# Gathered columns of a graph layer wait for TensorE's banks and picks of the preceding unit

## The chip, the cores and the metric

One Trainium2 chip; the kernel runs on one of its cores. The metric is the device time of one execution in microseconds (us), the median of several runs. Engines are named as the profile names them: PE is TensorE, DVE is VectorE, ACT is ScalarE, POOL is GpSimd, SP is SyncE.

## What is computed

A layer of a graph network over 6250 nodes with 64 features and 206250 edges, sorted by their target node. Cut to what matters:

```python
h = jnp.maximum(_layernorm(x, axis=-1), 0.0)
msg = jax.nn.relu(h[src] + edge_attr)          # 206250 x 64
agg = jax.ops.segment_sum(msg, dst, num_segments=6250)
out = x + (jax.nn.relu((h + agg) @ W1 + b1) @ W2 + b2)
```

The costly part is `h[src]`, one row of 64 floats for each edge, the rows in no order.

## The kernel before

**Groups and units.** The edges are worked through in groups of 768 (128 partitions, 6 columns of edges), 268 whole groups and a short last one. After a prologue (layer norm, ranks, the first five groups) a loop runs over 276 units, one call of `half(u)` each. A unit fetches the rows of `h` in two ways. Three of a group's six columns are gathered: POOL issues one indirect DMA for each column, 128 rows of 256 bytes from the table `h_rows` in memory to a tile `xg` (`gather`, line 200). The other three are picked by TensorE out of a copy of `h` that lies on the chip as three bf16 parts (`hp`). A few groups (`WHOLE`) have all six columns picked, in two units; they have no gathers.

**What a unit does on TensorE**, in this order: `window_sum(u - 1)` (line 600) sums the messages of the unit before into a bank, 12 small matmuls. `slots_of` (line 487) fills three slot banks for the next set of picks: two `first` ones and one `later`, of 20, 16 and 16 matmuls. `pick(u + 1)` (line 502) picks rows with 18 matmuls. ACT copies each slot bank out (`slots_out`, line 495), puts the edge attributes into the pick bank (`room`, line 510), and makes the messages (line 590). The DVE adds a finished sum into the accumulator `z` (line 563), adds the gathered rows to the edge attributes (line 585), adds the three picked parts up (line 588), compares for the one-hot tiles (line 569), and makes the selection matrices `backs` (line 474) and `found` (line 455) for later units.

**Order.** The order of the instructions on each engine is that of the program's text, without a scheduler. The framework puts semaphore waits where data or buffers need them. `enter(g + AHEAD)` at the start of a unit loads the group nine ahead (`AHEAD = 9`): its edge attributes by SP, its gathers by POOL. The gathered tiles come from a ring of twelve (`LOOK = 12`). POOL has nothing else to do in the loop, so what holds a gather there is the ring alone: the first column of a group waits for line 585 of the group that last used its buffer.

Of the kernel before, what the change touches and what calls it, by code (L numbers as in the profile page):

```python
# [21 lines left out]
G = 6  # L22
# [17 lines left out]
AHEAD = 9  # L40
# [4 lines left out]
H = 3  # L45
PP, RR = 128, 49
# [4 lines left out]
S = 32  # L51
J = P // S
assert PARTS * BB == RR - 1 and PP == P and PARTS % J == 0
Q = PARTS * S // P
# [3 lines left out]
RAW = 3  # L58
# [23 lines left out]
def kernel(  # L82
# [14 lines left out]
    nc = tc.nc  # L97
# [9 lines left out]
    src_sb = const.tile([P, CP], I32, name="src_sb")  # L107
# [70 lines left out]
    hp = const.tile([PP, RR, 3, D], BF16, name="hp")  # L178

    h_rows = dram.tile([NP, D], F32, name="h_rows")  # L180
# [8 lines left out]
    def attr_load(ea, g):  # L189
        if g < NG:  # L190
            nc.sync.dma_start(out=ea.rearrange("p j d -> p (j d)"),
                              in_=edge_attr[g * GE:(g + 1) * GE, :].rearrange("(p j) d -> p (j d)", j=G))
        else:
            nc.sync.dma_start(out=ea[:, G - CT:G - 1].rearrange("p j d -> p (j d)"),
                              in_=edge_attr[C * P:(C + TJ) * P, :].rearrange("(p j) d -> p (j d)", j=TJ))
            nc.sync.dma_start(out=ea[:, G - 1, :], in_=edge_attr[E - P:, :])

    def gather(xg, idx, n, rows):
        for j in range(n):
            nc.gpsimd.indirect_dma_start(  # L200
                out=xg[:, j, :], out_offset=None, in_=rows[:, :],
                in_offset=bass.IndirectOffsetOnAxis(ap=idx[:, j:j + 1], axis=0))

    def first_col(g):
        return 0 if g < NG else G - CT

    def is_whole(g):
        return g in WHOLE

    def pool_cols(g):  # L210
        return G if g < F0 else 0 if is_whole(g) else G - H

    def load(g):
        ea = eas[g % LOOK]
        attr_load(ea[:, :G], g)
        lo, hi = first_col(g), pool_cols(g)
        if is_whole(g):
            return ea, None
        if g < F0:
            xg = lnp.tile([P, G, D], F32, name="xr", bufs=F0)  # L220
        else:
            xg = edge.tile([P, G - H, D], F32, name="xg")
        gather(xg[:, lo:], src_sb[:, g * G + lo:g * G + hi], hi - lo, x if g < RAW else h_rows)
        return ea, xg

    loaded = [load(g) for g in range(RAW)]
    tail_load(dst_sb, dst_tail)
    tail_load(src_sb, src_tail)
# [113 lines left out]
    def next_half():  # L342
        halves_made[0] += 1
        return half_banks[halves_made[0] % 3]
# [94 lines left out]
    backs, sources, spots, found, picked, halves, picks = {}, {}, {}, {}, {}, {}, {}  # L439

    def source_load(k):
        sources[k] = rank.tile([P, PARTS * 2 * S], I16, name="sources")
        nc.sync.dma_start(out=sources[k][:PP], in_=lines[k // SETS][k % SETS].rearrange("(o m) s -> o (m s)", o=1)
                          .to_broadcast([PP, PARTS * 2 * S]))

    def spot_load(k):
        spots[k] = rank.tile([P, 2 * H * P], BF16, name="spots")
        nc.sync.dma_start(out=spots[k], in_=spot_rows[k * 2 * H:(k + 1) * 2 * H, :]
                          .rearrange("(o t) s -> o (t s)", o=1).to_broadcast([P, 2 * H * P]))
# [16 lines left out]
    def back_near(k):  # L466
        nc.scalar.activation(backs[k][:, Q - 1].rearrange("p t s -> p (t s)"), dists.pop(k), AF.Relu,  # L467
                             bias=ones[:, 0:1], scale=-1.0)
# [10 lines left out]
    def slots_of(k, n0):  # L479
        ps = next_half()[:, :2 * 3 * D].rearrange("p (u d) -> p u d", u=2)  # L480
        for u in range(2):
            i, q = divmod(n0 + u, Q)
            sets = BB + 1 if q == 0 else BB
            for b in range(sets):
                for j in range(J):
                    m = (b * PARTS + q * J) + j if b < BB else BB * PARTS + j
                    nc.tensor.matmul(ps[j * S:(j + 1) * S, u], found[k][:, m, i, :],  # L487
                                     hp[:, min(m, RR - 1)].rearrange("p t d -> p (t d)"),
                                     start=(b == 0), stop=(b == sets - 1))
        if n0 == 0:  # L490
            picked[k] = hot.tile([P, 2 * Q, 3 * D], BF16, name="picked")
        halves[k, n0] = ps

    def slots_out(k, n0):
        nc.scalar.copy(picked[k][:, n0:n0 + 2], halves.pop((k, n0)))  # L495

    def pick(u0, cols):
        k, i = divmod(u0, 2)
        ps = picks[u0]
        for u in cols:  # L500
            for q in range(Q):
                nc.tensor.matmul(ps[:, u, :3].rearrange("p t d -> p (t d)"), backs[k][:, q, i * H + u, :],  # L502
                                 picked[k][:, i * Q + q], start=False, stop=(q == Q - 1), skip_group_check=True)

    def room(u):
        g, c0 = UNITS[u]
        picks[u] = pick_banks[u % 2]
        parts = taken[g][0][:, H:].rearrange("p (t c) d -> p c t d", c=H)
        if c0:
            nc.scalar.copy(picks[u][:, :H, :3], parts)  # L510
        else:
            nc.scalar.copy(picks[u][:, :H, 0], taken[g][0][:, :H])
            nc.scalar.copy(picks[u][:, :H, 1:3], parts[:, :, 1:])

    def group_of(u):
        return UNITS[u][0] if u >= 0 else F0 + u
# [4 lines left out]
    def is_first(u):  # L521
        return u <= 0 or UNITS[u - 1][0] != UNITS[u][0]
# [24 lines left out]
    aggs, hots, taken, msgs = {}, {}, {}, {}  # L547
# [13 lines left out]
    def sum_into_z(u):  # L561
        at = window_start(group_of(u))
        nc.vector.tensor_tensor(z[:, ds(at, W)], z[:, ds(at, W)], aggs.pop(u), ALU.add)  # L563
# [7 lines left out]
            slots.unsqueeze(1).to_broadcast([P, n, W]), ALU.is_equal)  # L571
        hots[u] = oh

    def enter(g):
        if g <= NG and g not in taken:
            taken[g] = loaded[g] if g < RAW else load(g)

    def messages(u):
        g, (lo, hi) = group_of(u), span(u)
# [15 lines left out]
    def window_sum(u):  # L595
        (lo, hi), oh, msg = span(u), hots.pop(u), msgs.pop(u)
        pa = half_banks[u % 3][:, 2 * 3 * D + u // 3 % AB * W:][:, :W]
        for j in range(lo, hi):
            i = (j - lo) % 2
            nc.tensor.matmul(pa[i * D:(i + 1) * D], msg[:, j, :], oh[:, j, :], start=(j < lo + 2), stop=(j >= hi - 2))  # L600
        aggs[u] = pa
# [41 lines left out]
    def blocks_behind(u):  # L643
        g = group_of(u)
        for c in sorted(res):
            store(c, *res.pop(c))
        for c in sorted(hid):
            res[c] = result(c, *hid.pop(c))
        for c in range(NB):
            if READY[c] == g and is_last(u):  # L650
                hid[c] = hidden(c)
# [6 lines left out]
    def is_set(k):  # L658
        return 0 <= k < KS

    def half(u):
        g = group_of(u)
        k, i = divmod(u, 2)
        first = ((0, 2), (6, 8))[i]
        later = ((4,), (10,))[i]
        now = is_set(k + 1)
        if is_first(u):
            enter(g + AHEAD)
        if i == 0:
            if is_set(k + 3):  # L670
                source_load(k + 3)
        elif is_set(k + 3):
            spot_load(k + 3)
        window_sum(u - 1)
        if u + 1 < U:
            room(u + 1)
        if now:
            for n0 in first:
                slots_of(k + 1, n0)
                slots_out(k + 1, n0)  # L680
            for n0 in later:
                slots_of(k + 1, n0)
        if u + 1 < U:
            pick(u + 1, range(H))
        sum_into_z(u - LAG)
        blocks_behind(u - LAG)
        messages(u)
        if now:
            for n0 in later:
                slots_out(k + 1, n0)  # L690
        one_hot(u)
        if i == 0:
            if is_set(k + 1):
                back_near(k + 1)
                back(k + 1, 3, Q)
            if is_set(k + 2):
                find(k + 2, 0)
                find(k + 2, BB)
        else:
            if is_set(k + 2):  # L700
                back_far(k + 2)
                back(k + 2, 0, 3)
                find(k + 2, 1)
        chunk(u + 14, rank_at)
        chunk(u + 13, rank_count)
        chunk(u + 12, rank_of)
        chunk(u + 11, rank_marks)
        chunk(u + 11, rank_turn)
        chunk(u + 10, rank_holds)
        chunk(u + 10, rank_fits)  # L710
        chunk(u + 9, source)
        if g in CHECKS and is_first(u):
            find_left(CHECKS.index(g))
# [25 lines left out]
    heads, rows = [], []  # L739
# [80 lines left out]
    for u in range(U):  # L820
        half(u)
# [24 lines left out]
    with tc.If(any_left > 0):  # L846
        nc.gpsimd.iota(wide, pattern=[[1, WB]], base=1, channel_multiplier=0, allow_small_or_imprecise_dtypes=True)
        with tc.For_i(0, NG, 1) as i:
            idx = work.tile([P, G], I32, name="idx")
# [56 lines left out]
```

## Time and profile before

| | us |
|---|---|
| Median of 3 runs | 1706.47 |
| Lowest and highest | 1706.32, 1710.89 |
| The profiled execution | 1700.59 |
| Its span, first to last instruction | 1698.9 |
| Busy PE, DVE, ACT, POOL | 1226.6, 995.5, 954.9, 785.4 |

The mean granted clock of TensorE in the profile was 0.914. Busy time sums the lengths of an engine's instructions; a wait is put down to the engine that came last. "issue" is idle time in which the engine waited for nothing that the profile shows. In the timeline a row merges like instructions that follow each other: start, length, engine, line, operation, tiles, count, and in brackets the idle time before.

### The profile page before, as it was taken

To read this page: it belongs to the slowest core of one execution; us is meant where nothing else is said; L and a number is where in the kernel's file an instruction comes from. 1 tells how busy PE (TensorE), PEld (TensorE's weight loads), DVE (VectorE), ACT (ScalarE), POOL (GpSimd) and SP (SyncE) were. 2 spreads that over 40 slices of the span, in tenths; PEclk is the share of its full clock that TensorE was granted. 3 is DMA by queue.
4 is the path that set the end of the run, shared out by engine and by line. 5 is a ranking of instruction groups with operands and counts; after the bars stand their busy time and mean duration, and the time that the engine had idled before them with its cause. 6 is when DMAs were issued, how large, how long until landed. Compare 5 with 4: busy or idle time off the path is not lost. (4 is left out here: it accounts for less than half of the span.)

```text
span 1698.9 us, 54613 instructions
## 1 busy us (share of the span) xinstructions
PE 1226.6 (72%) x23185; PEld 957.5 (56%) x23185; DVE 995.5 (59%) x2686; ACT 954.9 (56%) x1979; POOL 785.4 (46%) x798
## 2 busy tenths in 40 slices
PE   3047777777777777877777777777777777777786
PEld 2036565655556566656556555655655565565665
DVE  7446556656566555655656555655556555565565
ACT  4335555556556555555655655655555555565664
POOL 6734544553453543554455454444444544545510
PEclk8569999899999998899999999988999999999998
DMA  5213433334333433334333433433334333434330
GB/s 182 70 51 104 110 96 105 108 96 111 102 97 107 112 104 93 107 94 118 105 104 102 109 103 98 105 106 103 96 102 106 98 106 106 109 98 109 106 95 25
DMA packets 115095, 172.34 MB, mean 101 GB/s; under 512 B 28444, under 2 KB 83613, under 8 KB 114845
## 3 DMA queue, kind: packets, MB, share of 16 engines
q1 hardware_dynamic: 89752, 143.03, 28.2%
q0 software_dynamic: 25088, 25.74, 8.5%
q8 instruction: 184, 3.01, 0.7%
q14 instruction: 67, 0.54, 0.1%
q10 hardware_dynamic: 4, 0.01, 0.0%
HBM read 164.85 MB, written 3.84 MB: 99 GB/s over the span
## 5 line engine op out<-in xcount | busy, mean ns | idle before, releaser
L200 POOL DMA_INDIRECT xg<-h_rows,src_sb x754 | 749.9, 995 | 827.6 <-DVE ea L585 662.4
L487 PE MATMUL half<-hp,found 128*32 128x192 bf16 x14352 | 509.6, 256 | 267.3 <-issue 243.3
L495 ACT CAST picked<-half 128x384 bf16<-128x384 f32 x828 | 365.2, 475 | 344.3 <-PE half L487 300.2
L487 PEld LDWEIGHTS <-found 128*32 128x32 bf16 x14352 | 325.2, 98 | 393.6 <-issue 357.1
L502 PE MATMUL pick<-picked,backs 128*128 128x192 bf16 x4968 | 519.1, 266 | 3.5 <-ACT pick L510 2.1
L502 PEld LDWEIGHTS <-backs 128*128 128x128 bf16 x4968 | 449.3, 106 | 60.5 <-issue 50.7
L563 DVE TENSOR_TENSOR z<-z,half 128x32 f32 x281 | 53.0, 189 | 638.4 <-ACT picked L495 511.1
L590 ACT ACTIVATE msg<-ea 128x384 f32<-128x384 f32 (+2 forms) x281 | 142.9, 509 | 259.2 <-DVE ea L588 199.1
L474 DVE TENSOR_SCALAR backs<-spots,ids 128x768 bf16<-128x768 int16 x690 | 279.9, 453 | 0.0
L600 PE MATMUL half<-oh,msg 128*64 128x32 f32 x3224 | 152.7, 229 | 109.5 <-ACT picked L495 57.5
L600 PEld LDWEIGHTS half<-oh,msg 128*64 128x64 f32 x3224 | 121.3, 140 | 171.8 <-ACT picked L495 75.1
L455 DVE TENSOR_SCALAR found<-sources,nodes_of 128x1536 bf16<-128x1536 int16 (+1 forms) x414 | 211.4, 537 | 0.1
L588 DVE TENSOR_REDUCE ea<-pick 128x192 f32<-128x576 f32 x276 | 207.1, 750 | 0.1
L510 ACT COPY pick<-ea 128x576 f32<-128x576 f32 x264 | 168.4, 638 | 0.0
L467 ACT ACTIVATE backs<-dist,ones 128x768 bf16<-128x768 bf16 x138 | 129.3, 937 | 0.3 <-ACT dist L464 0.3
L464 ACT ACTIVATE dist<-spots,far 128x768 bf16<-128x768 int16 x138 | 129.2, 936 | 0.0
L569 DVE TENSOR_TENSOR oh<-slot,slots 128x192 f32<-128x192 int16 (+2 forms) x281 | 95.4, 340 | 36.9 <-remote 36.9
L585 DVE TENSOR_TENSOR ea<-ea,xg 128x192 f32<-128x192 f32 x252 | 90.0, 357 | 1.8 <-issue 1.3
L279 PE MATMUL rows<-at,upper 128*128 128x432 f16 x46 | 16.5, 358 | 49.1 <-remote 28.4
L283 ACT CAST before<-rows 128x432 f16<-128x432 f32 x46 | 23.4, 510 | 35.7 <-remote 31.8
L331 PE MATMUL rows<-holds,marks 128*96 128x96 f16 x276 | 25.9, 232 | 11.4 <-DVE oh L569 5.0
L334 ACT CAST source<-rows 24x64 int16<-24x64 f32 x138 | 27.5, 199 | 8.5 <-remote 5.3
(107 smaller groups left out, 439.7 us busy)
## 6 DMA issues: line engine op xcount, KB each, us to landing
sources<-source_row SPq DMA_DIRECT2D x138, 384.0 KB
ea<-in_edge_attr_dram SPq DMA_DIRECT2D x268, 192.0 KB
spots<-spot_rows SPq DMA_DIRECT2D x138, 192.0 KB
xg<-h_rows,src_sb POOLq DMA_INDIRECT x754
xb<-in_x_dram SPq DMA_DIRECT2D x12, 128.0 KB
out_dram<-o SPq DMA_DIRECT2D x12, 128.0 KB
h_rows<-x SPq DMA_DIRECT2D x3, 384.0 KB
dst_sb<-in_dst_main_dram SPq DMA_DIRECT2D x1, 804.0 KB
```

What stands on the lines that cost most here:

```text
L200: nc.gpsimd.indirect_dma_start(out=xg[:, j, :], out_offset=None, in_=rows[:, :], in_offset=bass.IndirectOffsetOnAxis(ap=idx[:, j:j + 1], a ...
L455: nc.vector.tensor_scalar(found[k][:, b * PARTS:b * PARTS + n].rearrange("p m i s -> p (m i s)"), sources[k][:, :n * 2 * S], nodes_of[:, b ...
L464: nc.scalar.activation(dists[k], spots[k].bitcast(I16), AF.Abs, bias=far)
L467: nc.scalar.activation(backs[k][:, Q - 1].rearrange("p t s -> p (t s)"), dists.pop(k), AF.Relu, bias=ones[:, 0:1], scale=-1.0)
L474: nc.vector.tensor_scalar(backs[k][:, q].rearrange("p t s -> p (t s)"), spots[k].bitcast(I16), ids[:, q:q + 1], None, op0=ALU.is_equal)
L487: nc.tensor.matmul(ps[j * S:(j + 1) * S, u], found[k][:, m, i, :], hp[:, min(m, RR - 1)].rearrange("p t d -> p (t d)"), start=(b == 0), st ...
L495: nc.scalar.copy(picked[k][:, n0:n0 + 2], halves.pop((k, n0)))
L502: nc.tensor.matmul(ps[:, u, :3].rearrange("p t d -> p (t d)"), backs[k][:, q, i * H + u, :], picked[k][:, i * Q + q], start=False, stop=(q ...
L510: nc.scalar.copy(picks[u][:, :H, :3], parts)
L588: nc.vector.tensor_reduce(ea[:, c0:c0 + H], picks.pop(u)[:, :H, :3].rearrange("p j t d -> p j d t"), AX.X, ALU.add)
L590: nc.scalar.activation(msg[:, lo:hi], ea[:, lo:hi], AF.Relu)
L600: nc.tensor.matmul(pa[i * D:(i + 1) * D], msg[:, j, :], oh[:, j, :], start=(j < lo + 2), stop=(j >= hi - 2))
```

## The change

`gather` gets a list `behind` of TensorE instructions, and the last columns of its group each get a wait on one of them. The list `beats` grows by three instructions in each unit: the last matmul of the first slot bank, that of the later slot bank, and that of the picks. At the start of a unit the three that the preceding unit left go to `enter`. So of the group's three gathered columns the first waits for a slot bank of the preceding unit, the second for its later slot bank, the third for its picks. The waits that were there stay. The order of instructions on each engine is the same in the built program, and only POOL's gathers have new waits.

```diff
+    beats = []
+    beat = mybir.DependencyInfo(mybir.DependencyClass.Sync, mybir.DependencyReason.ANTI)
+
-    def gather(xg, idx, n, rows):
+    def gather(xg, idx, n, rows, behind=()):
         for j in range(n):
-            nc.gpsimd.indirect_dma_start(
+            it = nc.gpsimd.indirect_dma_start(
                 out=xg[:, j, :], out_offset=None, in_=rows[:, :],
                 in_offset=bass.IndirectOffsetOnAxis(ap=idx[:, j:j + 1], axis=0))
+            if j >= n - len(behind):
+                tc.add_manual_dep(it.ins, behind[j - n + len(behind)].ins.name, beat, reason="pace")
...
-    def enter(g):
+    def enter(g, behind=()):
         if g <= NG and g not in taken:
-            taken[g] = loaded[g] if g < RAW else load(g)
+            taken[g] = loaded[g] if g < RAW else load(g, behind[first_col(g):])
...
         if is_first(u):
-            enter(g + AHEAD)
+            enter(g + AHEAD, beats[-G + H:] if u > 0 else ())
...
         if now:
             for n0 in first:
-                slots_of(k + 1, n0)
+                begun = slots_of(k + 1, n0)
                 slots_out(k + 1, n0)
+                if n0 == first[0]:
+                    beats.append(begun)
             for n0 in later:
-                slots_of(k + 1, n0)
+                beats.append(slots_of(k + 1, n0))
         if u + 1 < U:
-            pick(u + 1, range(H))
+            beats.append(pick(u + 1, range(H)))
```

`slots_of` and `pick` return their last matmul for this.

More of the change, by code (lines that the diff above doesn't have):

```diff
@@ L211, in pool_cols, with load @@
         return G if g < F0 else 0 if is_whole(g) else G - H
-    def load(g):
+    def load(g, behind=()):
         ea = eas[g % LOOK]
@@ L222, in load @@
             xg = edge.tile([P, G - H, D], F32, name="xg")
-        gather(xg[:, lo:], src_sb[:, g * G + lo:g * G + hi], hi - lo, x if g < RAW else h_rows)
+        gather(xg[:, lo:], src_sb[:, g * G + lo:g * G + hi], hi - lo, x if g < RAW else h_rows, behind)
         return ea, xg
@@ L486, in slots_of @@
                     m = (b * PARTS + q * J) + j if b < BB else BB * PARTS + j
-                    nc.tensor.matmul(ps[j * S:(j + 1) * S, u], found[k][:, m, i, :],
-                                     hp[:, min(m, RR - 1)].rearrange("p t d -> p (t d)"),
-                                     start=(b == 0), stop=(b == sets - 1))
+                    last = nc.tensor.matmul(ps[j * S:(j + 1) * S, u], found[k][:, m, i, :],
+                                            hp[:, min(m, RR - 1)].rearrange("p t d -> p (t d)"),
+                                            start=(b == 0), stop=(b == sets - 1))
         if n0 == 0:
@@ L492, in slots_of @@
         halves[k, n0] = ps
+        return last
     def slots_out(k, n0):
@@ L501, in pick @@
             for q in range(Q):
-                nc.tensor.matmul(ps[:, u, :3].rearrange("p t d -> p (t d)"), backs[k][:, q, i * H + u, :],
-                                 picked[k][:, i * Q + q], start=False, stop=(q == Q - 1), skip_group_check=True)
+                last = nc.tensor.matmul(ps[:, u, :3].rearrange("p t d -> p (t d)"), backs[k][:, q, i * H + u, :],
+                                        picked[k][:, i * Q + q], start=False, stop=(q == Q - 1), skip_group_check=True)
+        return last
     def room(u):
```

## The prediction

> **What bounds the kernel now.** I read the page's busy times first, then the waits, then the timeline of one unit with gathers and of units without. Four rows of the waits give the outline (engine, tile and line, whom it waited for; us in total, times, longest):
>
> ```profile
> POOL xg L200 <- DVE ea L585: 662.4, 238, 21.2
> DVE z L563 <- ACT picked L495: 511.1, 213, 4.3
> ACT picked L495 <- PE half L487: 300.2, 206, 3.9
> PE half L487 <- issue: 243.3, 560, 1.2
> ```
>
> No engine is full. POOL waits for the DVE add of line 585, the DVE for ACT's copies of slot banks (line 495), ACT for TensorE's slot matmuls (line 487), and TensorE in the middle of these matmuls for nothing that the profile shows ("issue"). The page's groups give the number of each:
>
> ```profile
> L200 POOL DMA_INDIRECT xg<-h_rows,src_sb x754 | 749.9, 995 | 827.6 <-DVE ea L585 662.4
> L588 DVE TENSOR_REDUCE ea<-pick 128x192 f32<-128x576 f32 x276 | 207.1, 750 | 0.1
> ```
>
> There are 276 units, one reduction of line 588 each, and 754/3 = 251 of them have three gathers. A stretch of the timeline with gathers (start, length, both us; idle time before in brackets):
>
> ```profile
> 832.52 0.36 DVE L585 TENSOR_TENSOR ea<-ea,xg 128x192 f32<-128x192 f32 x1
> 832.79 0.75 DVE L588 TENSOR_REDUCE ea<-pick 128x192 f32<-128x576 f32 x1
> 833.14 0.94 POOL L200 DMA_INDIRECT xg<-h_rows,src_sb  x1 [2.10 <-DVE ea L585]
> 833.73 0.86 DVE L474 TENSOR_SCALAR backs<-spots,ids 128x768 bf16<-128x768 int16 x2
> 834.39 1.02 POOL L200 DMA_INDIRECT xg<-h_rows,src_sb  x1 [0.30 <-issue]
> 834.52 0.54 PE L600 MATMUL half<-oh,msg 128*64 128x32 f32 x12 [0.71 <-ACT picked L495]
> 834.99 1.23 PE L487 MATMUL half<-hp,found 128*32 128x192 bf16 x34
> 835.72 0.94 POOL L200 DMA_INDIRECT xg<-h_rows,src_sb  x1 [0.31 <-issue]
> 836.68 0.34 PE L487 MATMUL half<-hp,found 128*32 128x192 bf16 x6 [0.45 <-issue]
> 837.43 0.45 PE L487 MATMUL half<-hp,found 128*32 128x192 bf16 x12 [0.41 <-issue]
> 837.54 0.86 ACT L495 CAST picked<-half 128x384 bf16<-128x384 f32 x2 [1.70 <-PE half L487]
> 837.81 1.66 PE L502 MATMUL pick<-picked,backs 128*128 128x192 bf16 x18
> 838.43 0.19 DVE L563 TENSOR_TENSOR z<-z,half 128x32 f32 x1 [2.75 <-ACT picked L495]
> 838.61 0.36 DVE L585 TENSOR_TENSOR ea<-ea,xg 128x192 f32<-128x192 f32 x1
> 839.24 0.94 POOL L200 DMA_INDIRECT xg<-h_rows,src_sb  x1 [2.57 <-DVE ea L585]
> ...
> 843.60 0.86 ACT L495 CAST picked<-half 128x384 bf16<-128x384 f32 x2 [1.25 <-PE half L487]
> 844.39 0.75 DVE L588 TENSOR_REDUCE ea<-pick 128x192 f32<-128x576 f32 x1
> ```
>
> The same work near the end, where the last gather has been issued:
>
> ```profile
> 1641.16 0.75 DVE L588 TENSOR_REDUCE ea<-pick 128x192 f32<-128x576 f32 x1
> ...
> 1650.31 0.74 DVE L474 TENSOR_SCALAR backs<-spots,ids 128x768 bf16<-128x768 int16 x2
> 1651.20 1.26 PE L487 MATMUL half<-hp,found 128*32 128x192 bf16 x52
> ...
> 1652.35 0.85 ACT L495 CAST picked<-half 128x384 bf16<-128x384 f32 x2
> ...
> 1652.98 0.75 DVE L588 TENSOR_REDUCE ea<-pick 128x192 f32<-128x576 f32 x1
> ```
>
> With gathers two units take 844.39 - 832.79 = 11.60, so 5.80 each. Without, three units take 1652.98 - 1641.16 = 11.82, so 3.94. The three gathers thus cost 1.86 us a unit, and 251 x 1.86 = 467 us of the whole. Where it goes is seen on TensorE: 52 slot matmuls run in one piece of 1.26 us without gathers, and with them 34 run, then 6, then 12, with stops, the last from 4.29 us after the first gather (837.43 - 833.14). ACT's copies start together with that, 4.40 and, one unit on, 4.36 us after the first gather (837.54 - 833.14, 843.60 - 839.24), though the first bank's 20 matmuls are among the 34 that began at 834.99. So while POOL works off the three gathers, TensorE's supply of instructions and its signals are both held up.
>
> This closes a loop: first gather, 4.40 to the copies, 0.89 to the DVE's line 563 (838.43 - 837.54), 0.54 to the end of line 585 (838.97), 0.27 to the next first gather (839.24). Sum 6.10; with the other unit's 4.36 and shorter rest, 5.80 in the mean. POOL is released by line 585 alone, since its buffer ring is full, so the burst of three always lies in series with copies and add.
>
> **The change, part by part.** No instruction of TensorE, DVE, ACT or SP is added, taken away or moved. Three things are new.
>
> (1) Signals and waits: the pick matmuls that end a unit signal POOL (TensorE signals for banks anyway), and POOL takes one wait more for each of its columns. The 0.30 us between gathers of a burst bounds the handling from above if all of it were added, 3 x 0.30 = 0.9 us of POOL; below, nothing. POOL idles 827.6 us in front of its gathers, so I take nothing on the path: three gathers at 1.25 us apart (834.39 - 833.14) fill only 3.75 us of a unit.
>
> (2) Lead: gathers for nine groups ahead used to go out as soon as the ring of twelve had room; now they wait for TensorE one unit before their place, so the lead falls from twelve groups to between nine and ten. Behind a waiting gather only later gathers are queued; the attribute loads go by SP. The line that needs the data is line 585, still nine units of 5 us later, so no data is late. Three groups' gathers move from the prologue into units. Line 585 stops being what releases POOL: its buffer came free two units before.
>
> (3) Pacing, which decides. The first gather is released by the first slot bank (20 matmuls), the second by the third bank (all 52), the third by the end of the 18 picks. What a gather that stands alone does to TensorE isn't shown while slot matmuls run. One case is near: the very last gather.
>
> ```profile
> 1627.94 2.64 PE L502 MATMUL pick<-picked,backs 128*128 128x192 bf16 x18
> 1628.52 0.75 DVE L588 TENSOR_REDUCE ea<-pick 128x192 f32<-128x576 f32 x1
> 1628.87 0.95 POOL L200 DMA_INDIRECT xg<-h_rows,src_sb  x1 [2.33 <-DVE ea L585]
> ...
> 1633.11 0.75 DVE L588 TENSOR_REDUCE ea<-pick 128x192 f32<-128x576 f32 x1
> ```
>
> That unit took 4.59 us, 0.65 over 3.94, and its picks alone took 0.98 longer than 1.66. So the lower bound for a lone gather is nothing: a unit near 4.0. The upper bound: each gather holds TensorE for 4.29/3 = 1.43 us, and the next waits for a signal that is held until then, plus the 0.27 of release: 1.70 a gather, 5.10 for three, with TensorE's work beside it or not. If none of it were beside it, 12 sums (0.54) and 20 slot matmuls (20 x 1.26/52 = 0.48) come on top: 6.12.
>
> I take 5.3. The holding up is real in every unit, so I stay near the 5.10; on top I put 0.2, a fifth of the 1.02, because after the start at 834.52 twelve sums and most of 34 slot matmuls ran inside the held time, as TensorE had them already. The copies, line 563 and line 585 (1.43 us of the old loop) now lie beside the next gathers and not between. Next late is the loop of POOL and TensorE itself; the other loop, through ACT and DVE, needs 3.94.
>
> Sum: 251 x (5.80 - 5.30) = 126 saved, three more groups in units at 5.3 - 3.94 = 4 lost: 122. The profiled execution took 1700.59 us (span 1698.9), so 1578 by its own time; the median of the runs is 1706.47, so 1584. For 4.7 and 5.6 a unit the same gives 1433 and 1661: the own range of this case.
>
> A rule speaks against all this. The POOL row beside the DVE's binary compare is 1.02 instead of 0.94 us, and the compare 0.86 instead of 0.74. The Trainium skill, "SBUF — State Buffer", section "Who interferes with whom", has that case, an exclusive lock of the port pair between the DVE in a 2-port mode and GpSimd, and says "PE and ACT never wait on anyone." By it gathers would cost TensorE nothing wherever they stand. The stops within line 487 and the 3.94 against 5.80 disagree with that sentence here, though not with the lock.
>
> **The rivals.**
> - Slower. The signal that a gather waits for is held until the gather before it is worked off, and TensorE's supply with it, so that sums, banks and gathers run one after the other: 6.12, and 1706.5 + 251 x 0.32 + 6 = 1793. The place is between the third gather and the first bank of the next unit: with over 5.80 - 5.10 = 0.70 us of TensorE's work uncovered there the change loses. For it: the third gather starts at the end of the picks, just ahead of sums and first bank, which are in the long loop. Against: the 46 matmuls that ran at 834.52 and after.
> - Much faster. A lone gather holds nothing up, as around 1628.87: 4.1 a unit, 1706.5 - 251 x 1.70 = 1280. Against: the 34 matmuls were few enough to have been waiting ready, so this row may hide the same hold.
> - No change. What the gathers cost is the port lock alone and the 5.80 has another cause, say loads that go with them: moving them buys nothing, and 0.12 us of DVE per compare pair stays as it is: about 1706. Against: the units without gathers run the same compares and loads. The rule quoted from the Trainium skill stands behind this case.
> - The waits do nothing, since TensorE is always ahead of POOL. POOL now runs as far ahead as the ring lets it, two to three groups beyond the place where the new waits hold it, so they bind: I leave this no chance of its own.
>
> **How the numbers follow.** My case 0.62, slower 0.22, much faster 0.10, no change 0.06. Within 0.3% (5 us, about what a measurement can tell from none) lies "no change": 0.06. Faster: 0.62 + 0.10 = 0.72; slower 0.22. For the range I keep my case whole (down to 1433) and go upward through "no change" to 1745, about half-way to 1793; that leaves out nearly half of the slow case and the much faster one, together 2 in 10.
>
> **What would show it.** In the profile after: POOL's gathers no longer in bursts 1.25 us apart, released by TensorE's lines of banks and picks and not by line 585; the DVE's wait for ACT's copies well under 511 us; "issue" stops in line 487 fewer or shorter; reductions of line 588 some 5.3 us apart in units with gathers and still 3.9 without. Wrong it is if ACT's copies still start 4.4 us after a first gather, if the stops move to sums and first bank and units reach 5.8 or more, or if units come near 4, where a lone gather costs nothing.

## The result, and the profile after

The changed kernel took 1544.93 us (median of four runs, 1543.62 to 1545.83), the kernel before 1706.39 beside it. The ratio is 0.9053, with a 95% interval of 0.9028 to 0.9078. The forecast was 1584, faster, with an own range of 1433 to 1661. The profiled execution took 1545.8 us with a span of 1543.9, which is 155.0 less than the 1698.9 of before. TensorE's mean granted clock was 0.938 (0.914 before). Of the runs below, two had one slow execution among their four, which their ratios leave out: 2300.79 us for the run with the second first bank and 1361.49 for the run where only the second column waits.

First the busy times of the page, and two of its groups, the gathers and the slot matmuls:

```profile
PE 1134.9 (74%) x23185; PEld 920.1 (60%) x23185; DVE 980.2 (63%) x2686; ACT 951.6 (62%) x1979; POOL 781.5 (51%) x798
...
L204 POOL DMA_INDIRECT xg<-h_rows,src_sb x754 | 747.4, 991 | 693.6 <-PE half L493 571.5
...
L493 PE MATMUL half<-hp,found 128*32 128x192 bf16 x14352 | 439.8, 256 | 110.2 <-issue 58.9
```

POOL does the same work (754 gathers, 991 ns each after 995), and what ends its idle time is now TensorE's slot matmuls (line 493, line 487 before) and no longer the DVE's add. The answer of the waits (total us, times, longest):

```profile
POOL xg L204 <- PE half L493: 571.5, 472, 23.6
DVE z L571 <- ACT picked L502: 436.5, 215, 4.2
...
ACT picked L502 <- PE half L493: 103.9, 172, 3.4
...
PE half L493 <- issue: 58.9, 166, 1.2
...
POOL xg L204 <- PE pick L509: 27.3, 26, 3.0
```

Three rows fell: ACT's wait for the banks from 300.2 to 103.9 us, TensorE's stops inside the slot matmuls from 243.3 to 58.9, the DVE's wait for ACT's copies from 511.1 to 436.5. The last row is new, and small: the picks are seldom what holds the third gather. What is left of two of the rows is best judged by a run shown further down, in which no gather is left (line 566 is the add there, line 498 the copies):

```profile
DVE z L566 <- ACT picked L498: 258.6, 185, 3.6
...
ACT picked L498 <- PE half L490: 10.1, 19, 3.9
```

There the DVE waits 258.6 us for ACT's copies and ACT 10.1 us for the banks, and the stops inside the slot matmuls come to 0.3 us. So of the DVE's 511.1 us about half goes with the gathers, and 178 us of that are still there after the change.

The timeline of three units after (start, length, both us; idle time before in brackets), with only the lines that carry the loop:

```profile
834.30 1.26 PE L493 MATMUL half<-hp,found 128*32 128x192 bf16 x52
835.18 0.94 POOL L204 DMA_INDIRECT xg<-h_rows,src_sb  x1 [1.25 <-PE half L493]
835.45 0.85 ACT L502 CAST picked<-half 128x384 bf16<-128x384 f32 x2
...
836.37 0.75 DVE L596 TENSOR_REDUCE ea<-pick 128x192 f32<-128x576 f32 x1
836.91 0.94 POOL L204 DMA_INDIRECT xg<-h_rows,src_sb  x1 [0.79 <-PE half L493]
...
837.59 0.46 ACT L502 CAST picked<-half 128x384 bf16<-128x384 f32 x1
...
838.16 1.03 POOL L204 DMA_INDIRECT xg<-h_rows,src_sb  x1 [0.30 <-issue]
838.57 1.89 PE L493 MATMUL half<-hp,found 128*32 128x192 bf16 x52
...
840.23 0.95 POOL L204 DMA_INDIRECT xg<-h_rows,src_sb  x1 [1.04 <-PE half L493]
...
841.27 0.75 DVE L596 TENSOR_REDUCE ea<-pick 128x192 f32<-128x576 f32 x1
841.94 0.94 POOL L204 DMA_INDIRECT xg<-h_rows,src_sb  x1 [0.76 <-PE half L493]
...
843.19 1.22 POOL L204 DMA_INDIRECT xg<-h_rows,src_sb  x1 [0.31 <-issue]
...
845.02 0.86 ACT L502 CAST picked<-half 128x384 bf16<-128x384 f32 x2 [0.70 <-PE half L493]
845.26 0.95 POOL L204 DMA_INDIRECT xg<-h_rows,src_sb  x1 [0.86 <-PE half L493]
846.75 0.19 DVE L571 TENSOR_TENSOR z<-z,half 128x32 f32 x1 [2.41 <-ACT picked L502]
846.92 0.94 POOL L204 DMA_INDIRECT xg<-h_rows,src_sb  x1 [0.72 <-PE half L493]
847.24 0.74 DVE L596 TENSOR_REDUCE ea<-pick 128x192 f32<-128x576 f32 x1
```

Three things are to be seen.

- The second gather starts 1.73, 1.71 and 1.66 us after the first (835.18 to 836.91, 840.23 to 841.94, 845.26 to 846.92), although the later bank it waits for is the last of 52 matmuls that at 834.30 were over at 835.56. Two gathers that wait for nothing are 1.25 us apart, so POOL could have started the first of these second gathers at 836.43. It started 0.48 us after that, and 1.35 us after the bank's end: the bank's signal came late. Of the 251 gaps from a first to a second gather 234 are 1.65 to 1.75 us long in the trace, and none was before the change.
- The third gather follows the second at 1.25, with "issue": when POOL is ready for it, the picks have signalled. So the three are no longer one burst. In the trace both gaps of a group were under 1.5 us in 249 of 251 groups before, and in 10 after.
- At 845.02 two bank copies run on ACT and are over at 845.88, but the DVE's line 571 (line 563 before), which waits for one, starts at 846.75, 1.49 after the gather at 845.26. While a gather that stands alone is worked off, ACT's signal to the DVE comes late too, here by 0.87 us. It is no single case: 69 of the 281 adds of this line start 0.80 to 0.95 us after the last copy was over, each of them 1.48 to 1.54 us after the start of a gather, and without gathers none of them does.

The reductions of line 596 lie 4.90 and 5.97 us apart here (836.37, 841.27, 847.24), and a pattern of three units, about 4.0 to 4.5, 5.1 and 5.9, repeats through much of the loop. Over the 250 intervals between the first 251 reductions the mean is 5.204 us ((1412.91 - 112.03)/250, from the starts in the trace), before 5.778.

### The profile page after: what moved, and what is told of

Read it like the earlier page. It is cut to its first block, busy times and chain, and to the rows that moved or that the text cites. A ratio compares the mean times of both kernels' runs of the same rounds, so it can differ in the third digit from the quotient of the medians.

```text
span 1543.9 us, 55101 instructions
## 1 busy us (share of the span) xinstructions
PE 1134.9 (74%) x23185; PEld 920.1 (60%) x23185; DVE 980.2 (63%) x2686; ACT 951.6 (62%) x1979; POOL 781.5 (51%) x798
## 2 busy tenths in 40 slices
DMA packets 115098, 172.36 MB, mean 112 GB/s; under 512 B 28444, under 2 KB 83613, under 8 KB 114845
## 5 line engine op out<-in xcount | busy, mean ns | idle before, releaser
L493 PE MATMUL half<-hp,found 128*32 128x192 bf16 x14352 | 439.8, 256 | 110.2 <-issue 58.9
L509 PE MATMUL pick<-picked,backs 128*128 128x192 bf16 x4968 | 490.7, 257 | 3.4 <-ACT pick L518 3.3
L509 PEld LDWEIGHTS <-backs 128*128 128x128 bf16 x4968 | 425.0, 102 | 54.7 <-issue 50.3
L502 ACT CAST picked<-half 128x384 bf16<-128x384 f32 x828 | 366.0, 475 | 106.2 <-PE half L493 103.9
L493 PEld LDWEIGHTS <-found 128*32 128x32 bf16 x14352 | 312.0, 99 | 182.5 <-issue 101.3
L571 DVE TENSOR_TENSOR z<-z,half 128x32 f32 x281 | 52.9, 188 | 506.3 <-ACT picked L502 436.5
L480 DVE TENSOR_SCALAR backs<-spots,ids 128x768 bf16<-128x768 int16 x690 | 259.1, 424 | 0.0
L461 DVE TENSOR_SCALAR found<-sources,nodes_of 128x1536 bf16<-128x1536 int16 (+1 forms) x414 | 198.6, 506 | 0.1
L593 DVE TENSOR_TENSOR ea<-ea,xg 128x192 f32<-128x192 f32 x252 | 93.7, 372 | 2.1 <-issue 1.7
```

What stands on the lines that cost most here:

```text
L461: nc.vector.tensor_scalar(found[k][:, b * PARTS:b * PARTS + n].rearrange("p m i s -> p (m i s)"), sources[k][:, :n * 2 * S], nodes_of[:, b ...
L480: nc.vector.tensor_scalar(backs[k][:, q].rearrange("p t s -> p (t s)"), spots[k].bitcast(I16), ids[:, q:q + 1], None, op0=ALU.is_equal)
L493: last = nc.tensor.matmul(ps[j * S:(j + 1) * S, u], found[k][:, m, i, :], hp[:, min(m, RR - 1)].rearrange("p t d -> p (t d)"), start=(b == ...
L509: last = nc.tensor.matmul(ps[:, u, :3].rearrange("p t d -> p (t d)"), backs[k][:, q, i * H + u, :], picked[k][:, i * Q + q], start=False, ...
```

## The experiments

The runs were made on three chips, and the kernel before was timed beside them on each. The first chip takes 1702.75 us for it (13 runs), the second 1672.97 (7 runs), the third 1310.86 (7 runs). Ratios are to the kernel before on the same chip. On which chip the changed kernel itself was timed is not known; its 1706.39 us for the kernel before is closest to the first chip's. It was not timed beside the runs of the second and third chip, so where a ratio of those is set beside its 0.9053, the comparison may go across chips.

**First chip: does pacing do it, or the start of the burst; and do bytes or gathers cost?**

Only the first column waits, for the first bank; the other two follow in a burst.

```diff
-            if j >= n - len(behind):
-                tc.add_manual_dep(it.ins, behind[j - n + len(behind)].ins.name, beat, reason="pace")
+            if behind and j == 0:
+                tc.add_manual_dep(it.ins, behind[0].ins.name, beat, reason="pace")
```

> From the changed kernel, only the first of a group's three columns waits for TensorE (its first slot bank); the other two follow at once, in a burst. Theory (the burst in series behind the DVE's add was the cost, and a burst holds TensorE's signals from about 2 us to 4.4 us after its first gather): the burst now lies beside copies, add and message, the next first bank's signal is held to 4.4 us after it, so units of 4.7 to 5.2 us, 1430 to 1560 us in all. Rival (the spacing inside the unit is what pays): a burst stays a burst, units near 5.6 to 5.8, 1650 to 1710 us.

Measured: 1715.88 us, ratio 1.0069 (1.0040 to 1.0097). The theory failed, and the rival's range was 6 us short. The whole gain is gone: to move the burst off the DVE's add buys nothing, so the gain needs the waits of the other columns. The timeline of one unit shows what is late instead:

```profile
834.97 0.95 POOL L204 DMA_INDIRECT xg<-h_rows,src_sb  x1 [1.96 <-PE half L493]
...
836.22 0.95 POOL L204 DMA_INDIRECT xg<-h_rows,src_sb  x1 [0.30 <-issue]
...
837.47 0.95 POOL L204 DMA_INDIRECT xg<-h_rows,src_sb  x1 [0.30 <-issue]
838.85 0.64 PEld L608 LDWEIGHTS half<-oh,msg 128*64 128x64 f32 x12 [0.30 <-issue]
...
839.32 0.48 ACT L502 CAST picked<-half 128x384 bf16<-128x384 f32 x1 [1.46 <-PE rows L287]
```

The copy of the later bank starts at 839.32, 4.35 us after the first gather of the burst, the same 4.4 as before the change. ACT's instructions run in the order of the program's text, so what follows this copy on ACT, the next unit's bank copies among it, stands behind it.

The same burst, but behind the picks (`behind[-1]` in place of `behind[0]`):

> From the changed kernel, the first column waits for the picks of the preceding unit and the other two follow at once. Theory (it decides which signals of the long loop the held time covers): the burst now starts just ahead of sums and first bank and holds the first banks' signals for some 4.3 us, then 52 slot matmuls and 18 picks follow: units of 6 to 6.6 us, 1750 to 1900 us. Rival (any release other than the DVE's add will do): as the changed kernel, 1530 to 1570 us.

Measured: 1900.10 us, ratio 1.1168 (1.1138 to 1.1198). The theory holds, at the upper end of its range. The waits show TensorE's stops back (247.1 us, before the change 243.3) and longer waits of ACT and the DVE than before it:

```profile
DVE z L571 <- ACT picked L502: 627.7, 184, 5.6
ACT picked L502 <- remote: 423.6, 189, 4.0
PEld L493 <- issue: 367.9, 622, 1.3
...
PE half L493 <- issue: 247.1, 549, 1.2
```

So a burst behind one wait can cost 0.7% or 12% over the kernel before, by what it then covers: here sums, first banks and their copies.

The kernel before, with all three gathers of a unit replaced by loads of SP:

```diff
+            if rows is h_rows and n <= H and j >= 0:
+                nc.sync.dma_start(out=xg[:, j, :], in_=rows[j * P:(j + 1) * P, :])
+                continue
```

> From the kernel before, the gathers of the units are replaced by plain loads of as many rows of the same table by SP (the first 384 rows, so wrong rows are added). Theory (what holds TensorE is POOL's working off of a gather, not the bytes): units of 3.9 to 4.2 us, 1230 to 1310 us. Rival (the rows' transfers in small pieces hold it): units near 5.8, about 1700 us.

Measured: 1288.71 us, ratio 0.7576 (0.7549 to 0.7603), as the theory had it. As many bytes by another way cost 414 us less, 35 us of it ahead of the first reduction. The plain loads are not the larger pieces: the page counts 124955 packets under 512 bytes, and 28444 with gathers. So neither the bytes nor small packets are the cost. What differs besides is that the rows are no longer picked by index, and that POOL no longer works; this run doesn't separate these.

One gather left, by `j >= 1` in place of `j >= 0`:

> From the kernel before, only the first column of a group is gathered by POOL, the other two are plain loads by SP (wrong rows in those two). Theory (one gather holds 1.4 us, and alone it falls beside the message): units of 4.0 to 4.6 us, 1250 to 1410 us. Rival (each gather costs a third of the 1.86 us wherever it falls): 4.56 us, 1395 us. Rival (bytes): about 1700 us.

Measured: 1312.31 us, ratio 0.7715 (0.7692 to 0.7738), 23.6 us above none, where the rival had 1395. One gather for each unit costs 0.09 us a unit at that place, so the cost of three, 414 us, is no sum of single costs. The timeline shows a lone gather ahead of slot matmuls that run in one piece:

```profile
735.32 0.94 POOL L203 DMA_INDIRECT xg<-h_rows,src_sb  x1 [3.61 <-DVE ea L588]
...
736.80 1.26 PE L490 MATMUL half<-hp,found 128*32 128x192 bf16 x52
```

The slot matmuls start 1.48 us after the gather, about when the DVE's late adds above start as well, so little of its hold falls on them.

**Second chip: which of the waits does the work, and is there a better place?** On this chip the run without the third wait stands in for the changed kernel.

The third column's wait is left out (`and j < H - 1` added to the condition `j >= n - len(behind)`):

> The changed kernel, but the third column waits for nothing of TensorE (the first for the first bank, the second for the later bank). In the changed kernel the third gather follows the second at 1.25 us in most units and the picks end its idle time for 27.3 us in all. Theory (the wait that does the work is the second column's: it keeps the second gather from starting before the later bank's signal is through): the same as the changed kernel within 1%, 1530 to 1560. Rival (each of the three waits carries a third of the gain): some 50 us back towards the kernel before, 1590 to 1610.

Measured: 1515.67 us, ratio 0.9073 (0.9043 to 0.9103), against 0.9053 for the change, with intervals that overlap. The theory holds as far as this comparison goes: the picks' wait does nothing that can be seen.

The second column's wait is left out (`and j != 1`):

> The changed kernel, but the second column waits for nothing of TensorE: it starts 1.25 us after the first, and the third waits for the picks of the preceding unit. Theory (a gather that is being worked off holds the other engines' signals, a second one right behind lengthens the hold, and the later bank's copy is then late and ScalarE stands in it): much of the gain is lost, 1600 to 1720. Rival (it is enough that the three are not all in one burst): 1530 to 1570.

Measured: 1582.34 us, ratio 0.9454 (0.9424 to 0.9484); 58% of the gain is left (0.0546 of 0.0947; of the 0.0927 of the run before it on this chip 59%). In ratios the theory's 1600 to 1720 over 1706 are 0.938 to 1.008, so the size is inside, at the mild end. Its mechanism is not the one seen. ACT doesn't stand in its copies longer than in the changed kernel (100.1 us of idle time before line 502, there 106.2). The DVE does wait longer:

```profile
DVE z L571 <- issue: 265.1, 81, 5.0
DVE z L571 <- ACT picked L502: 247.0, 135, 4.2
```

```profile
833.86 0.85 ACT L502 CAST picked<-half 128x384 bf16<-128x384 f32 x2
...
834.24 0.94 POOL L204 DMA_INDIRECT xg<-h_rows,src_sb  x1 [0.30 <-PE half L493]
...
835.49 0.94 POOL L204 DMA_INDIRECT xg<-h_rows,src_sb  x1 [0.30 <-issue]
836.32 0.19 DVE L571 TENSOR_TENSOR z<-z,half 128x32 f32 x1 [3.02 <-issue]
```

The two copies are over at 834.71; the DVE's add starts at 836.32, 1.61 later and 2.08 after the first gather of a pair. "issue" stands here where the copies had been over for more than 1 us, so the two rows belong together: 512.1 us, and 471.7 in the changed kernel (436.5 and 35.2).

The first column waits for the second of the two first banks, by a change of one index (`n0 == first[1]` in place of `first[0]`):

> The changed kernel, but the first column waits for the second of the two first slot banks instead of the first of them, some 0.5 us later; the others as they are. Theory (a lone gather holds signals from some 0.6 us after its start to 1.65 us, and in a third of the units what falls there is the copies' signal to the one-hots of VectorE, 2.41 us of wait in the units of 5.9 us): the copies' signal passes ahead of the hold, the units of 5.9 us fall to 5.1 to 5.4, 1440 to 1530. Rival (the gathers' total working time sets the unit, wherever they start): the same within 1%, 1530 to 1560. Against both: the third column then reaches into the next unit's window sums, and it is 1560 to 1650.

Measured: 1501.22 us, ratio 0.8970 (0.8936 to 0.9005), the fastest of the forms with waits on the first two chips. The step expected is there: of the first 250 units 63 took 5.7 to 6.2 us in the changed kernel and 6 here, and

```profile
DVE z L571 <- ACT picked L502: 256.0, 142, 4.6
...
DVE z L571 <- issue: 127.7, 78, 3.6
```

the DVE's wait for ACT's copies fell from 436.5 to 256.0, about what it is without gathers (258.6). But 92.5 us of it were given back as "issue" (35.2 to 127.7) and 62.7 as a wait for the copy into the pick bank (line 518, 4.1 to 66.8). The units under 4.2 us went as well, from 36 to 14: the gain over the changed kernel is 0.9% (0.8970 over 0.9053), where the theory had 1 to 7% and the rival "the same within 1%". By time the run doesn't decide between them: the late signal of ACT is gone, and the hold has moved onto other signals more than it has gone.

The gathers show something else:

```profile
809.67 0.94 POOL L204 DMA_INDIRECT xg<-h_rows,src_sb  x1 [0.65 <-PE half L493]
...
810.92 1.08 POOL L204 DMA_INDIRECT xg<-h_rows,src_sb  x1 [0.31 <-issue]
...
812.77 1.12 POOL L204 DMA_INDIRECT xg<-h_rows,src_sb  x1 [0.77 <-DVE found L461]
```

The second gather follows the first at 1.25 us here and in 248 of 251 groups, just as in the run without the second wait (247), and the third follows some 1.9 us later (there 2.0). With much the same spacing one run has a ratio of 0.8970 and the other of 0.9454. So the distance between gathers is not what decides. What differs is where the pair starts, behind the second first bank or behind the first, and so which signals are still to come.

Each wait one event later, for the later bank, the picks and the next unit's window sums (`beats[-5:-2]`, with `beats.append(window_sum(u - 1))` in place of the first bank):

> The changed kernel, but each column waits one event later: for the later bank, the picks, and the window sums of the unit after, so that no gather starts between the first banks and the later bank. Theory (what counts is which signals fall in the 0.6 to 1.65 us behind a gather's start): the copies of the first two banks are free of the hold, the third bank's too, but the first gather then stands over the picks and the third over the next first bank, whose copies open the next unit: 1500 to 1700, no nearer. Rival (spacing by signals of TensorE is all that counts, whichever they are): 1530 to 1570.

Measured: 1520.24 us, ratio 0.9102 (0.9066 to 0.9139). 0.9102 of 1706 is 1553, inside the rival's range, and inside the wider one of the theory, so the run doesn't separate them. The three runs on this chip in which the second column waits for TensorE lie within 1.3% of the kernel before (0.8970 to 0.9102).

**Third chip: no hold to be tested.** Four runs were to take the hold apart further. On this chip the kernel before itself takes 1310.86 us, as much as with one gather on the first chip. It was not profiled there; the profiles of that chip are those of the four runs.

Two gathers in a burst and one load of SP (`j >= 2`):

> The kernel before, but of a unit's three columns two are gathered, in a burst as before, and the third comes by a plain load of as many rows (other rows than the reference's). With no gather it was 1289, with one 1312, with three 1703. Theory (gathers right behind each other lengthen one hold, to 4.4 us behind the first for three, so to some 3.1 us for two, each behind the one ahead by 1.25 us; the copies then come 1.25 us sooner and the unit of 5.80 us falls to 4.3 to 4.6): 1380 to 1460. Rival (beyond the first each gather costs the same): 1312 + 195 = 1507, 1490 to 1530.

Measured: 1302.89 us, ratio 0.9936 (0.9920 to 0.9953). Inconclusive: with the kernel before at 1310.86 there is no hold for a further gather to lengthen.

The gathers behind ACT's copies (`slots_out` returns its copy, `beats` gets that of `first[1]` and that of `later`):

> The changed kernel, but the gathers wait for ScalarE and not for TensorE: the first for the copy of the second slot bank, the second for the copy of the later bank, the third for nothing. Theory (a gather that waits for a signal lets that signal pass first; the copies' signal opens the one-hots' add on VectorE, which waits 436.5 us for it in the changed kernel): that wait falls by half or more, the hold moves to the message and the window sums, 1470 to 1540. Rival (only signals of TensorE matter): the hold falls on the next first bank, 1600 to 1700. Rival (any spacing does): 1530 to 1570.

Measured: 1303.81 us, ratio 0.9943 (0.9926 to 0.9959). Inconclusive for the same reason.

Only the second column waits, for the later bank (`and j == 1`):

> The changed kernel, but only the second column waits, for the later bank; the first and the third wait for nothing of TensorE. Theory (the second column's wait does the work, since it keeps the second gather from starting before the later bank's signal is through): within 3% of the changed kernel, 1530 to 1590. Rival (two waits are needed, the first holds the first gather off the sums): 1610 to 1710.

Measured: 1305.57 us, ratio 0.9939 (0.9920 to 0.9959). As a test of the waits inconclusive, but its timeline shows the same burst without the hold:

```profile
700.27 0.94 POOL L204 DMA_INDIRECT xg<-h_rows,src_sb  x1 [0.70 <-PE half L493]
...
701.52 0.97 POOL L204 DMA_INDIRECT xg<-h_rows,src_sb  x1 [0.30 <-issue]
...
702.48 1.26 PE L493 MATMUL half<-hp,found 128*32 128x192 bf16 x52
...
702.79 0.95 POOL L204 DMA_INDIRECT xg<-h_rows,src_sb  x1 [0.30 <-issue]
...
703.63 0.85 ACT L502 CAST picked<-half 128x384 bf16<-128x384 f32 x2
```

Three gathers 1.25 and 1.27 us apart, 52 matmuls in one piece among them, and copies 3.36 us after the first gather and 1.15 after the matmuls' start, as in the units without gathers that the prediction shows (1652.35 - 1651.20). ACT's copies wait for TensorE 11.5 us in all, not 300.2, though the gathers are as many and as long:

```profile
L204 POOL DMA_INDIRECT xg<-h_rows,src_sb x754 | 755.3, 1002 | 448.0 <-PE half L493 266.8
...
L502 ACT CAST picked<-half 128x384 bf16<-128x384 f32 x828 | 364.5, 475 | 14.0 <-PE half L493 11.5
```

Nine iotas of GpSimd for each unit in place of the three gathers:

```diff
+            if rows is h_rows and n <= H and j >= 0:
+                for _ in range(3):
+                    nc.gpsimd.iota(xg[:, j, :], pattern=[[1, D]], base=0, channel_multiplier=0, allow_small_or_imprecise_dtypes=True)
+                continue
```

> The kernel before, but each gather of a unit is replaced by three iotas of GpSimd that write the column (numbers instead of the rows), some 1 us a column by the 583 ns of a 128x96 iota, at the same place and behind the same wait. Theory (what holds the others up is the gather's being worked off, not GpSimd's being busy): as with plain loads, 1260 to 1310. Rival (GpSimd at work beside VectorE does it, whatever it does): 1550 to 1710.

Measured: 1290.67 us, ratio 0.9846 (0.9830 to 0.9863). Inconclusive as to the hold. It shows that where the others aren't held up the gathers cost 20 us more than the iotas (1310.86 - 1290.67). Whether iotas would hold the others up on the first two chips stays untested, so the rival, GpSimd at work whatever it does, stands there.

## Why the prediction was right

The forecast was right in sign and, at 39 us too much, in size. By its own steps:

**What bounds.** Right that the burst is the cost, and that it holds TensorE's signals up. The loads of SP show the cost of the gathers by itself. Right only in part that the series with copies and add is the reason: with the burst released by the first bank and not by the add, the 250 units were no shorter (5.872 us in the mean, before 5.778). The cost is smaller than the prediction's, since the unit without gathers was taken from the last few, 3.94 us. Over the same 250 intervals the kernel without gathers has a mean of 4.346, so the gathers cost 1.43 us a unit and not 1.86, and 414 us in all, prologue included, not 467. The sum did not use that term but for the 4 us of the moved groups.

**Handling of the new waits.** Taken at nothing, and nothing speaks against that: the third gather, which has a new wait, follows the second at 1.25 us as before, a gather takes 991 ns on POOL and took 995, and without the third wait the ratio is 0.9073, on the second chip.

**Lead.** Right: line 593 ended one of POOL's waits, 2.1 us, where line 585 had ended 238, so the ring no longer holds the gathers. No data was late, for line 593 itself sat idle 2.1 us in all. Where the prediction had 4 us lost for three groups that move from the prologue into units (29 gathers instead of 36 go out ahead of the first reduction), that reduction, of line 596, came 6.7 us sooner (at 112.03 us, before 118.77).

**Pacing.** Right in the sum, wrong in its parts. The prediction put three gathers at 1.70 us each, 5.10, and 0.2 on top. Measured between the gathers of the last 200 units: median 1.70 from first to second, as forecast; 1.25 from second to third, since the picks' signal had come by the time POOL was ready; 2.08 from the third to the next first, which waits for sums and the first bank of the next unit. Together 5.03, and 5.204 as the mean of the 250 units, where 5.3 was taken. That the two errors, 0.45 too much in one gap and 0.38 too little in another, nearly cancel is luck. The 0.2 on top was chosen and not worked out, so the nearness of the 5.3 is in part luck too. So these 250 units gave 143.6 us, the last 25 intervals 4.5, the prologue 6.7 and what follows the last reduction 0.2: the 155.0 of the span, where the sum had 126 - 4 = 122. Of the 39 us by which the forecast was too high 33 are this, 17.6 by the unit (143.6 for 126), 10.7 by the prologue (a gain of 6.7 for a loss of 4), 4.5 by the last intervals. The other 6 are the profiled execution of before, which lay 5.9 under the median on which the forecast was put. TensorE's granted clock rose beside it, from 0.914 to 0.938, and a pick matmul took 257 ns and not 266; what share of the unit that is, no run separates.

**What the prediction did not name.** That a burst placed elsewhere is no better (1.0069 behind the first bank, 1.1168 behind the picks): in the unit shown of the first of these runs it is the later bank's copy, in ACT's order, that is late; how much of the time is this copy's no run separates. The second column's wait matters, for without it about 42% of the gain goes, but there it is the DVE's add that starts late and seldom that copy. Nor did the prediction name the signal from ACT to the DVE, which a lone gather holds as well. It goes with the units of 5.9 us: 59 of the 69 late adds lie in units of 5.7 to 6.2 us, and in the run with the second first bank both are nearly gone (no late add, 6 such units). And the prediction took the loop through ACT and DVE to need 3.94 us and to be out of the way, where the DVE still waits 178 us more for ACT's copies than without gathers.

**The rivals.** "No change", by which the port lock alone is the cost, is refuted: on the first chip TensorE's stops inside the slot matmuls fall from 243.3 to 0.3 us with loads of SP in place of the gathers and 414 us go, far more than compares 0.1 us shorter can give; on the second, waits alone give 5 to 10%. The sentence of the Trainium skill that stood behind it, "PE and ACT never wait on anyone." ("SBUF — State Buffer", section "Who interferes with whom"), does not foretell what happens beside gathers on those two chips, where TensorE stops and ACT waits; that it is a port they wait for, which is what the section is about, no run shows. On the third, 11.5 us of ACT's wait for the banks agree with the sentence. "Much faster", a lone gather free, holds for one gather at a harmless place (0.09 us a unit) and not for three that each wait for a signal of TensorE. "Slower" needed more than 0.70 us of TensorE's work uncovered between a third gather and the next first bank. The gap there is 2.08 us, 0.38 over the 1.70 of a gather, so the rival was near, and the gap from second to third gave back 0.45 of its 1.70.

**What was to be seen.** Bursts: groups with both gaps under 1.5 us went from 249 to 10, but second and third gather still follow each other at 1.25 us in most units (188 of 251 gaps under 1.3). Releaser, stops in line 487 and the DVE's wait went as said; the last fell only from 511.1 to 436.5, and "well under" was too much.

**Open.** What the hold is, is not shown, nor whether it comes from POOL's work or from the gather's transfers. The runs show whom it hits (TensorE inside its matmuls, with nothing that the profile shows it to wait for, TensorE's signals to ACT and POOL, ACT's to the DVE) and how long: some 1.5 to 1.7 us after the start of a lone gather, 4.3 to 4.6 after the first of three (181 of the 186 bank copies that waited over 0.3 us in the kernel before, from the 51st group of gathers on). That one gather lengthens the hold of the one before it is argued from these numbers; the run with two gathers was to show it and ran on a chip without a hold. What differs between the chips the profile does not show: number, length and bytes of the gathers are the same. The changed kernel itself was not timed beside the runs of the third chip.

## What to carry to other kernels

When an engine stops in the middle of its own instructions with nothing to wait for, look at what another engine is issuing at that time, and price it by taking that out and putting the same bytes on another queue (here 414 us). Where short disturbances run together, place each behind a signal that must get through, and ask which signals are still to come while it lasts. Distance alone is not the aim: with two gathers 1.25 us apart one run here was the fastest and another lost 42% of the gain. Some of the waits may be idle. And time the kernel before on the chip on which the variant runs: a change of this kind gave 9.5% on one chip, and on another its variants gave 0.6%.

## What the runs showed of the hardware that was not expected

- The same program took 1702.75, 1672.97 and 1310.86 us on three chips, the last with a granted clock of 0.962 to 0.968. On the first two the gathers hold other engines up; on the third no such hold shows (ACT waits 11.5 us for the banks, and 10.1 without gathers on the first).
- On the first two, signals of other engines come late beside an indirect gather of 128 rows that POOL shows as 0.94 us long: the engine that waits starts some 1.5 to 1.7 us after the gather's start. With three that follow each other at 1.25 to 1.4 us ACT's copies start 4.3 to 4.6 us after the first, shown on the first.
- On the first chip one gather a unit cost 23.6 us over the whole kernel, and three in a burst 414. With the change's waits three cost 1545 - 1289 = 256.
